# Final element's output projection in token halves with one PSUM bank for a block, and two output blocks between scores as row halves of the array

## The chip, the cores and the metric

The kernel runs on one core of a Trainium2 chip, in f32 throughout. The core has five engines that each run their own queue of instructions in program order: TensorE (PE; its weight loads are shown as PEld), VectorE (DVE), ScalarE (ACT), GpSimd (POOL) and SyncE (SP, which here only issues DMAs). The metric is the device time of one execution in microseconds (us); a kernel's time is the median of its runs.

## What is computed

The input is x with 8 batch elements of 512 channels and 32 x 32 = 1024 tokens. Two attention layers follow one another, each element on its own:

```python
# layer 0
hn  = group_norm(x, 32 groups)
q, k, v = split(w_qkv @ hn + b_qkv)            # 8 heads of 64 channels
wgt = softmax(q^T k / sqrt(64))                # 1024 x 1024 for each head
a   = wgt applied to v
x   = x + group_norm(w_proj @ a + b_proj)
# layer 1
q, k, v = split(weight_norm(v_qkv) @ x)        # each token normalised by its RMS over q, k and v
e   = exp(scores of q and k)                   # one head of 512 channels, 1024 x 1024
h   = (v applied to e) / sum(e)
out = (x + weight_norm(v_out) @ h) / sqrt(2)
```

## The kernel before

**Tiles.** Channels lie on the partitions: 512 channels are 4 blocks (`CI`) of `P` = 128 rows, and the 1024 tokens are two halves of `HN` = 512 or 8 blocks (`NT`) of 128. Each element passes through layer 0 in `STEPS` = 32 steps, a step being the scores of two heads for one token block, and then through layer 1 (`Layer1`, from line 912). `B` = 8 elements run one after the other.

**PSUM.** Two pools hold matmul results: three buffers of two banks (`wide`, and the scores) and two buffers of one bank (`bank`). A bank is 128 x 512 f32. A tile is taken from a pool in rotation, so a matmul into a new tile waits until the tile that had the buffer two or three takes ago has been read. In the rows of the profile `s` are score tiles, `pq` and `pqk` the projections of q and k, `po` outputs of attention (of both layers), `pp` the final element's output projection, `py` the products with the Gram matrix at the start of layer 1.

**Big buffers in SBUF.** Seven large slots are handed out first come, first served. `big(name)` takes one and `slots.give(name)` gives it back. Weight buffers that change owner with the stage are `near[name]`; `place(name, b)` takes such a place again and `fetch` issues its load on SP.

**Order.** Each engine's instructions stay in the order in which the program issues them, so the order of the Python calls is the order of the work. All operations go through one helper, which is why every row of the profile says L34.

**One step of layer 0** (`Heads.step`, line 630): `softmax(i)` (VectorE takes the negated maximum `nm` of both score tiles, ScalarE the exponential `p`), then every second step `values` of five steps ago, then the calls in `fill`, then the scores of the next step, then `turn` (VectorE transposes the scaled p of the step before into `pb`, and SP issues four DMAs that move it into `pT`), then `scale` (VectorE reciprocal, GpSimd two multiplications of p), then the calls in `later`. What `fill` holds is therefore TensorE work placed between two sets of scores. Score matmuls, and the projections called pq, use half of the array's rows each: two matmuls with 64 rows of contraction, one on the upper half of the rows and one on the lower. The output blocks `po` of layer 1 use all 128 rows.

**The passage from one element to the next.** The last part of layer 1 multiplies v by e for the second half of the tokens: four blocks of 128 channels, `products(1, c)` (line 1076), each eight logical matmuls into one bank. `keep(1, c)` (line 1085) follows: VectorE multiplies the bank by `sums`, the reciprocals of the exponentials' sums, then adds x times 2^-0.5 and stores into x, and SP sends the block out. Block 0 is done before the next element's heads begin. Blocks 1, 2 and 3 are handed to the first steps of the next element's heads: `fills` (line 1386) puts `products(1, c)` ahead of the scores of the step, `laters` (line 1387) puts `keep(1, c)` at its end. This happens seven times. Where there is a next element, the multiplication's result `share` lies in SBUF (`near["v#"]`), in the rows called `t` or `v`.

**The last element's layer 0.** There is no next element that could fill the gaps. While the last heads run, `project_out_half` (line 651) puts the projection of the first two channel blocks of `a` plus bias into `o`. After the loop of 32 steps (lines 1326 to 1340) come `values(14)`, `heads.turn()` with the last transpose and its DMAs, the load of the scores' weights, `OutBegun` (line 660), which starts the third channel block's share of the projection (ci = 2) for three of four output blocks in two-bank tiles, two loads of x, `values(15)`, and `finish_last` (line 671). The latter adds the fourth channel block's share (ci = 3) and finishes the remaining output block. For each output block, both token halves at once, it adds the tile to o (VectorE), takes statistics (two `bn_stats`) and aggregates them. Then it fetches `gram`, forms the GroupNorm coefficients a and c in a chain of small steps, and for each channel block ScalarE scales o and VectorE adds it to x. Layer 1's `project` (line 912) follows with py.

**The end.** After the last element's layer 1 the four blocks `products(1, c)` and `keep(1, c)` run in a row, without heads beside them (line 1395); here the multiplication's result stays in PSUM. Each block is sent with one DMA of 512 KB.

Of the kernel before, what the change touches and what calls it, by code (L numbers as in the profile page):

```python
# [18 lines left out]
G1S, G1B, BQ, BK, BV, BP, G2S, G2B, GQKV, GOUT, NCOLS = 0, 4, 8, 12, 16, 20, 24, 28, 32, 44, 48  # L19
# [33 lines left out]
def attention_blocks_kernel(  # L53
# [36 lines left out]
    ov = out.rearrange("b (ci p) h w -> b p ci (h w)", p=P)  # L90

    const = ctx.enter_context(tc.tile_pool(name="const", bufs=1))
    slots = Slots(ctx.enter_context(tc.tile_pool(name="slots", bufs=1)), "s", 7)
# [5 lines left out]
    small = ctx.enter_context(tc.tile_pool(name="small", bufs=3))  # L99
    tiny = ctx.enter_context(tc.tile_pool(name="tiny", bufs=1))  # L100
# [4 lines left out]
    PE, VE, AC, PO, SY = (InOrder(tc, e) for e in (nc.tensor, nc.vector, nc.scalar, nc.gpsimd, nc.sync))  # L105
# [5 lines left out]
    def wide(name):  # L111
        return ps_s.tile([P, 2, HN], F32, tag="sc", name=name)
# [4 lines left out]
    def matmuls(pm, terms):  # L117

        for k, (lhsT, rhs) in enumerate(terms):
            PE.matmul(pm, lhsT, rhs, start=(k == 0), stop=(k == len(terms) - 1))  # L120
            if k % 2:
                yield

    def run(pieces):
        for _ in pieces:
            pass
# [24 lines left out]
    def load_x(b, xt, ci):  # L151
        SY.dma_start(out=xt[:, ci, :], in_=xv[b, :, ci, :])
# [116 lines left out]
    def fetch(name, b):  # L269
        SY.dma_start(out=place(name, b), in_=far[name])  # L270
# [16 lines left out]
    def gn_stats(st, src, k):  # L287
        VE.bn_stats(st[:, k, :], src[:, k * HN : (k + 1) * HN])

    class GroupNorm:  # L290


        def __init__(self, mv, n, g0, b0, name, bank=bank):
            self.mv, self.n, self.g0, self.b0, self.name, self.bank = mv, n, g0, b0, name, bank
# [352 lines left out]
    def out_terms(a, j, th, cis):  # L647
        hs = slice(th * HN, (th + 1) * HN)
        return [(near["proj"][:, ci, j * P : (j + 1) * P], a[:, ci, hs]) for ci in cis]
# [7 lines left out]
                AC.activation(o[:, j, th * HN : (th + 1) * HN], pm, AF.Identity, bias=col(BP, j))  # L657
            yield

    class OutBegun:  # L660


        def __init__(self, b, h):
            self.pm = {}
            for j in range(CI - 1):
                self.pm[j] = wide(f"pp_{b}_{j}")
                for th in range(2):
                    for lhsT, rhs in out_terms(h.a, j, th, [CI // 2]):
                        PE.matmul(self.pm[j][:, th, :], lhsT, rhs, start=True, stop=False)

    def finish_last(b, h, xt, o, begun):

        def project_out(j, th, pm):
            terms = out_terms(h.a, j, th, range(CI // 2, CI))
            if j in begun.pm:
                PE.matmul(pm[:, th, :], *terms[1], start=False, stop=True)
            else:
                run(matmuls(pm[:, th, :], terms))  # L680

        st = tiny.tile([P, CI, 2, 6], F32, tag="gn_st2", name=f"st2_{b}")
        mv = small.tile([P, CI, 2], F32, tag="gn_mv2", name=f"mv2_{b}")
        for j in range(CI):
            pm = begun.pm[j] if j in begun.pm else wide(f"pp_{b}_{j}")
            for th in range(2):
                project_out(j, th, pm)
            VE.tensor_add(o[:, j, :], o[:, j, :], pm.rearrange("p a f -> p (a f)"))
            for k in range(2):
                gn_stats(st[:, j], o[:, j, :], k)  # L690
            VE.bn_aggr(mv[:, j, :], st[:, j])
        fetch("gram", b)
        norm = GroupNorm(mv, CI, G2S, G2B, f"2_{b}")
        norm.means()
        a, c = norm.coeffs()
        for j in range(CI):
            AC.activation(o[:, j, :], o[:, j, :], AF.Identity, bias=c[:, j : j + 1], scale=a[:, j : j + 1])
            VE.tensor_add(xt[:, j, :], xt[:, j, :], o[:, j, :])
        slots.give(f"a_{b}")
        slots.give(f"o_{b}")  # L700

    class RightSide:

# [197 lines left out]
    class Layer1:  # L901
# [174 lines left out]
        def products(self, th, c, between=None, po=None):  # L1076
# [4 lines left out]
            for k, _ in enumerate(matmuls(po, terms)):  # L1081
                if k == 1 and between:
                    between()

        def keep(self, th, c):

            hs = slice(th * HN, (th + 1) * HN)

            po = self.po.pop((th, c))
            share = near["v#"][:, N : N + HN] if self.b + 1 < B else po  # L1090
            VE.tensor_mul(share, po, self.sums[:, hs])
            VE.scalar_tensor_tensor(self.xt[:, c, hs], self.xt[:, c, hs], 2.0 ** -0.5, share, ALU.mult, ALU.add)
            if th == 1:
                SY.dma_start(out=ov[self.b, :, c, :], in_=self.xt[:, c, :])

# [135 lines left out]
    for b in range(B):  # L1231
# [77 lines left out]
        if more:  # L1309
            v0_next = big(f"v0_{b + 1}", NT)  # L1310
            v0 = project_v7(b + 1, right_v.columns, v0_next)
            Seven.hold()
            for _ in range(4):
                next(v0)
        heads.values(STEPS // RG - 2)
        heads.turn()
        if more:
            Seven.drain()
            fetch("proj7", b)
            ta = big(f"ta_{b}").rearrange("p (k i) (h n) -> p k i h n", k=2, h=2)  # L1320
            rhs = RightSide(heads.a, ta[:, 0], ta[:, 1])
            for j in range(CI // 2 + 1):
                rhs.sums(j)
            for _ in range(10):
                next(v0)
        else:
            fetch("score", b)
            begun = OutBegun(b, heads)
            for ci in (2, 3):
                load_x(b, xt, ci)  # L1330
        heads.values(STEPS // RG - 1)
        slots.give(f"v0_{b}")
        if more:
            xt = big(f"x_{b}")
            for ci in range(CI):
                load_x(b, xt, ci)
            fetch("gram", b)
            finish_layer0(b, heads, rhs, xt, v0)
        else:
            finish_last(b, heads, xt, o_last, begun)  # L1340
        fetch("value", b)
        one = Layer1(b, xt)
        one.project(hn_next)
# [36 lines left out]
        if more:  # L1380
            one.products(1, 0, norm_step)
            run(steps)
            one.keep(1, 0)
            heads = Heads(b + 1, hn_now, v0_next, qk_next)
            heads.scores(0)
            fills = [[lambda c=c: one.products(1, c)] for c in range(1, CI)] + [[]]
            laters = [[lambda c=c: one.keep(1, c)] for c in range(1, CI)] + [[]]

            def done(b=b):
                for name in (f"v1_{b}", f"e_{b}_1", f"x_{b}"):  # L1390
                    slots.give(name)

            laters[CI - 2].append(done)
        else:
            for c in range(CI):
                one.products(1, c)
                one.keep(1, c)


# [31 lines left out]
```

## Time and profile before

| | us |
|---|---|
| median of the 3 runs | 3225.41 (3222.88 to 3227.68) |
| the profiled execution's own time | 3224.11 |
| its span, from the first to the last instruction | 3222.0 |
| TensorE busy in it | 3192.6 |
| VectorE / GpSimd / ScalarE busy in it | 2279.2 / 1253.2 / 1045.5 |
| idle of TensorE before po<-pT,v, released by DMA pT<-pb | 3.0 |
| last TensorE instruction ends at | 3216.83 |

The mean TensorE clock granted in the span is 0.998 of full. A row of the profile names engine, operation, `out<-in` by the program's names with buffer numbers left out, the form (partitions x elements), and the count; a matmul's `64*128 64x512` is rows of contraction x output partitions, and the moving operand. One logical f32 matmul shows as two records on PE. Because matmuls are pipelined, a record's length overlaps the next record: the time from start to start is what a matmul costs. In a timeline the columns are start, busy time, engine, operation; a bracket gives the idle time before it and what ended that. Instructions of the same group that follow one another are put together, with x and their number.

### The profile page before, as it was taken

What the parts mean: (1) busy time and instruction counts of PE and PEld (TensorE: products, weight loads), DVE (VectorE), ACT (ScalarE), POOL (GpSimd) and SP (SyncE); (2) the same over time, 40 slices, a digit from 0 to 9 for tenths busy, and PEclk for the clock granted to TensorE, in tenths of its full rate; (3) what the DMA queues carried; (4) which work ended last, traced back from release to release, by engine and by line L of the source; (5) the groups of instructions that cost most, each with busy time, mean ns of one, the idle gap of its engine ahead of it and who ended that gap; (6) DMA issues with size and microseconds to landing.
All of it is one profiled execution on the core that took longest, in us unless ns stands there. A gap on an engine that the chain in (4) does not pass through costs nothing.

```text
span 3222.0 us, 36603 instructions
## 1 busy us (share of the span) xinstructions
PE 3192.6 (99%) x13218; PEld 1645.9 (51%) x13218; DVE 2279.2 (71%) x3166; ACT 1045.5 (32%) x1813; POOL 1253.2 (39%) x1025
## 2 busy tenths in 40 slices
PE   8999999999999999999999999999999999999899
PEld 5455644455444554545544555445554556444354
DVE  5697767876678765886658866587766877578652
ACT  2453114521145211551215512254023531145210
POOL 1554224732257212671227613265223642246121
PEclk9999999999999999999999999999999999999999
DMA  6777225862168512784228832388224872158600
GB/s 203 206 204 219 76 56 155 215 200 59 56 182 226 179 43 62 203 229 142 53 85 213 224 111 52 107 215 235 92 58 112 216 220 75 30 156 211 187 7 33
DMA packets 225180, 451.57 MB, mean 140 GB/s; under 512 B 21572, under 2 KB 62056, under 8 KB 219112
## 3 DMA queue, kind: packets, MB, share of 16 engines
q1 hardware_dynamic: 224880, 449.20, 49.7%
q8 instruction: 106, 1.74, 0.2%
q14 instruction: 74, 0.61, 0.1%
q10 hardware_dynamic: 120, 0.02, 0.0%
HBM read 137.26 MB, written 29.56 MB: 52 GB/s over the span
## 4 chain that ended last, share of the span: by engine, by line
PE 93%; DMA 3%; DVE 2%; SPq 1%; issue 1%; POOL 1%; DVEq 0%; ACTq 0%; POOLq 0%
PE po L34 26%; PE s L34 13%; PE pq L34 7%; PE p_e_T L34 7%; PE p_v_T L34 6%; PE p_e_B L34 5%; PE p_v_B L34 5%; PE pqk L34 4%; PE py L34 4%; PE p_u_T L34 3%; PE p_o_T L34 3%; PE p_u_B L34 3%; PE p_o_B L34 2%; DMA pT<-pb 2%; DVE pb L34 1%; PE pv L34 1%
## 5 line engine op out<-in xcount | busy, mean ns | idle before, releaser
L34 POOL TENSOR_SCALAR p<-p,tt 128x1024 f32<-128x1024 f32 x512 | 566.0, 1118 | 742.0 <-DVE tt L34 729.6
L34 ACT ACTIVATE p<-s,nm 128x1024 f32<-128x1024 f32 x512 | 565.6, 1109 | 876.3 <-DVE nm L34 534.0
L34 DVE TENSOR_REDUCE nm<-s 128x1 f32<-128x1024 f32 x512 | 602.2, 1217 | 151.7 <-PE s L34 151.0
L34 DVE STREAM_TRANSPOSE pb<-p 128x2048 f32<-128x2048 f32 x256 | 589.9, 2304 | 50.3 <-DMA pT<-pb 27.8
L34 PE MATMUL s<-qk 64*128 64x512 f32 x2048 | 524.0, 604 | 1.1 <-POOL qk L34 0.5
L34 PE MATMUL po<-pT,v 128*64 128x256 f32 x4096 | 471.8, 383 | 3.1 <-DMA pT<-pb 3.0
L34 PE MATMUL po<-e,v 128*128 128x512 f32 x1024 | 450.8, 596 | 0.0
L34 PEld LDWEIGHTS po<-pT,v 128*64 128x64 f32 x4096 | 285.1, 137 | 221.0 <-ACT v L34 31.8
L34 PEld LDWEIGHTS s<-qk 64*128 64x128 f32 x2048 | 200.5, 186 | 250.7 <-issue 222.2
L34 PEld LDWEIGHTS po<-e,v 128*128 128x128 f32 x1024 | 191.4, 190 | 241.1 <-issue 241.1
L34 PE MATMUL pq<-hn,qk 64*128 64x512 f32 x504 | 197.1, 592 | 0.0
L34 POOL TENSOR_TENSOR esum<-esum,e 128x512 f32<-128x512 f32 x96 | 130.5, 1360 | 154.3 <-ACT e L34 151.8
L34 POOL TENSOR_TENSOR u<-u,xy 128x512 f32<-128x512 f32 x64 | 79.2, 1268 | 280.9 <-DMA xy<-far_rinv 275.4
L34 POOL TENSOR_TENSOR x<-x,o 128x1024 f32<-128x1024 f32 x21 | 52.1, 2512 | 348.5 <-ACT o L34 348.5
L34 ACT ACTIVATE e<-e,shift,rinv 128x512 f32<-128x512 f32 x128 | 100.9, 812 | 256.7 <-DVE e L34 256.7
L34 DVE TENSOR_TENSOR e<-e,p_e_T 128x512 f32<-128x512 f32 x160 | 107.0, 685 | 86.5 <-PE p_e_T L34 84.3
L34 DVE TENSOR_TENSOR v<-v,p_v_T 128x256 f32<-128x256 f32 x300 | 114.3, 417 | 68.7 <-PE p_v_T L34 50.0
L34 PE MATMUL pqk<-hn,qk 64*128 64x512 f32 (+1 forms) x672 | 158.2, 590 | 0.0
L34 PE MATMUL pq<-v,qk 64*128 64x512 f32 x336 | 150.9, 589 | 0.0
L34 PE MATMUL pq<-t,qk 64*128 64x512 f32 x336 | 150.9, 589 | 0.0
L34 PE MATMUL p_e_T<-s,t 128*128 128x512 f32 x320 | 147.8, 592 | 0.0
L34 PE MATMUL py<-x,gram 128*128 128x512 f32 x320 | 140.3, 598 | 5.4 <-issue 5.4
(222 smaller groups left out, 4096.7 us busy)
## 6 DMA issues: line engine op xcount, KB each, us to landing
pT<-pb SPq DMA_DIRECT2D x1024, 256.0 KB, 4.6
qk<-far_qk SPq DMA_DIRECT2D x21, 896.0 KB
hn<-in_x_dram SPq DMA_DIRECT2D x32, 512.0 KB, 4.6
x<-in_x_dram SPq DMA_DIRECT2D x32, 512.0 KB, 3.6
out_dram<-x SPq DMA_DIRECT2D x32, 512.0 KB, 4.6
score<-far_score SPq DMA_DIRECT2D x8, 1792.0 KB
value<-far_value SPq DMA_DIRECT2D x8, 1792.0 KB
proj<-far_proj SPq DMA_DIRECT2D x7, 1792.0 KB
```

The costliest lines, as they stand in the source:

```text
L34: return lambda *args, **kw: self._pin(call(*args, **kw))
```

## The change

There are three parts.

**1. Row halves.** For the seven passages to a next element, blocks 2 and 3 of `products(1, c)` become `products_rows(c)`. Each matmul is split by rows of contraction: the upper 64 rows accumulate into one bank, the lower 64 into a second one, so that the block has 16 logical matmuls of 64 rows in place of 8 of 128, in the same form as the scores. `keep` then has two results to add: the first as before, the second by a ScalarE copy to SBUF and two GpSimd operations, a multiplication by `sums` and an addition into x. The output's DMA comes after that. Block 1 is unchanged.

**2. The last element's output projection in token halves.** `LastOut` takes the place of `OutBegun` and `finish_last`. Each output block of each token half has a bank of its own: half 0 in two tiles of two banks, half 1 in a tile of two banks and two tiles that use one of theirs. `first_half` runs both remaining channel blocks (ci = 2 and 3) for token half 0 right after the loop, ahead of `values(14)`, and `sums(0, 0)` (add, one `bn_stats`) stands ahead of `heads.turn()`. After the turn come the other three sums of half 0, and `begin_second` (ci = 2, half 1); after `values(15)`, `finish` adds ci = 3, with sums and aggregation for each block. `gram` gets a big slot of its own and is loaded earlier; the loads of x stand ahead of that of the scores' weights, which moves behind them. The last step over o and x runs in token halves.

**3. The last block of the last element.** Its first 512 columns, finished earlier, are sent before it; its second 512 columns are done in two pieces of 256 columns (`last_piece`), each with its own matmuls, its own multiplication and addition, and its own DMA of 128 KB.

```diff
-    class OutBegun:
+    class LastOut:
+        def __init__(self, b, h, o):
+            self.b, self.h, self.o = b, h, o
...
             self.pm = {}
-            for j in range(CI - 1):
-                self.pm[j] = wide(f"pp_{b}_{j}")
+        def banks(self, th, groups):
+            for js in groups:
+                t = wide(f"pp_{self.b}_{th}_{js[0]}")
+                for k, j in enumerate(js):
+                    self.pm[th, j] = t[:, k]
+        def share(self, th, j, ci, first):
+            for lhsT, rhs in out_terms(self.h.a, j, th, [ci]):
+                PE.matmul(self.pm[th, j], lhsT, rhs, start=first, stop=not first)
+        def first_half(self):
+            self.banks(0, ((0, 1), (2, 3)))
+            for j in range(CI):
+                self.share(0, j, CI - 2, True)
+                self.share(0, j, CI - 1, False)
+        def sums(self, th, j):
+            oh = self.o[:, j, th * HN : (th + 1) * HN]
+            VE.tensor_add(oh, oh, self.pm[th, j])
+            VE.bn_stats(self.st[:, j, th, :], oh)
+        def begin_second(self):
+            self.banks(1, ((0, 3), (1,), (2,)))
+            for j in range(CI):
+                self.share(1, j, CI - 2, True)
+        def finish(self, xt):
+            b, o = self.b, self.o
+            for j in range(CI):
+                self.share(1, j, CI - 1, False)
+                self.sums(1, j)
+                VE.bn_aggr(self.mv[:, j, :], self.st[:, j])
+            norm = GroupNorm(self.mv, CI, G2S, G2B, f"2_{b}")
+            norm.means()
+            a, c = norm.coeffs()
+            for j in range(CI):
                 for th in range(2):
-                    for lhsT, rhs in out_terms(h.a, j, th, [CI // 2]):
-                        PE.matmul(self.pm[j][:, th, :], lhsT, rhs, start=True, stop=False)
-    def finish_last(b, h, xt, o, begun):
...
-            VE.tensor_add(o[:, j, :], o[:, j, :], pm.rearrange("p a f -> p (a f)"))
-            for k in range(2):
-                gn_stats(st[:, j], o[:, j, :], k)
-            VE.bn_aggr(mv[:, j, :], st[:, j])
-        fetch("gram", b)
...
-            AC.activation(o[:, j, :], o[:, j, :], AF.Identity, bias=c[:, j : j + 1], scale=a[:, j : j + 1])
-            VE.tensor_add(xt[:, j, :], xt[:, j, :], o[:, j, :])
+                    hs = slice(th * HN, (th + 1) * HN)
+                    AC.activation(
+                        o[:, j, hs], o[:, j, hs], AF.Identity, bias=c[:, j : j + 1], scale=a[:, j : j + 1]
+                    )
+                    VE.tensor_add(xt[:, j, hs], xt[:, j, hs], o[:, j, hs])
...
+        def products_rows(self, c):
+            pos = self.po[1, c] = [bank(f"po1_{self.b}_1_{c}_{r}") for r in range(2)]
+            for t in range(NT):
+                for r in range(2):
+                    rows = halves[r]
+                    PE.matmul(
+                        pos[r],
+                        self.v[rows, t, c * P : (c + 1) * P],
+                        self.e[1][rows, t, :],
+                        start=(t == 0),
+                        stop=(t == NT - 1),
+                    )
         def keep(self, th, c):
-            po = self.po.pop((th, c))
+            po, rest = self.po.pop((th, c)), None
+            if isinstance(po, list):
+                po, rest = po
...
+            if rest is not None:
+                part = near["v#"][:, :HN]
+                AC.copy(part, rest)
+                PO.tensor_mul(part, part, self.sums[:, hs])
+                PO.tensor_add(self.xt[:, c, hs], self.xt[:, c, hs], part)
             if th == 1:
                 SY.dma_start(out=ov[self.b, :, c, :], in_=self.xt[:, c, :])
+        def last_piece(self, c, cols):
+            hs, po = slice(HN + cols.start, HN + cols.stop), bank(f"po1_{self.b}_1_{c}_{cols.start}", HN // 2)
+            run(matmuls(po, [(self.v[:, t, c * P : (c + 1) * P], self.e[1][:, t, cols]) for t in range(NT)]))
+            VE.tensor_mul(po, po, self.sums[:, hs])
+            VE.scalar_tensor_tensor(self.xt[:, c, hs], self.xt[:, c, hs], 2.0 ** -0.5, po, ALU.mult, ALU.add)
+            SY.dma_start(out=ov[self.b, :, c, hs], in_=self.xt[:, c, hs])
...
+        else:
+            last = LastOut(b, heads, o_last)
+            last.first_half()
+            last.sums(0, 0)
         heads.values(STEPS // RG - 2)
         heads.turn()
...
-            fetch("score", b)
-            begun = OutBegun(b, heads)
+            for j in range(1, CI):
+                last.sums(0, j)
+            last.begin_second()
+            near["gram"] = big(f"gram_{b}")[:, :, :C]
+            SY.dma_start(out=near["gram"], in_=far["gram"])
             for ci in (2, 3):
                 load_x(b, xt, ci)
+            fetch("score", b)
         heads.values(STEPS // RG - 1)
...
-            fills = [[lambda c=c: one.products(1, c)] for c in range(1, CI)] + [[]]
+            fills = [[lambda c=c: (one.products_rows(c) if c > 1 else one.products(1, c))] for c in range(1, CI)] + [[]]
...
-            for c in range(CI):
+            for c in range(CI - 1):
                 one.products(1, c)
                 one.keep(1, c)
+            SY.dma_start(out=ov[b, :, c + 1, :HN], in_=xt[:, c + 1, :HN])
+            for n in (0, HN // 2):
+                one.last_piece(c + 1, slice(n, n + HN // 2))
```

More of the change, by code (lines that the diff above doesn't have):

```diff
@@ L658, in project_out_half @@
             yield
-    class OutBegun:
-        def __init__(self, b, h):
-            self.pm = {}
-            for j in range(CI - 1):
-                self.pm[j] = wide(f"pp_{b}_{j}")
-                for th in range(2):
-                    for lhsT, rhs in out_terms(h.a, j, th, [CI // 2]):
-                        PE.matmul(self.pm[j][:, th, :], lhsT, rhs, start=True, stop=False)
-    def finish_last(b, h, xt, o, begun):
[L675 to L687, printed above, removed]
-            VE.tensor_add(o[:, j, :], o[:, j, :], pm.rearrange("p a f -> p (a f)"))
-            for k in range(2):
-                gn_stats(st[:, j], o[:, j, :], k)
-            VE.bn_aggr(mv[:, j, :], st[:, j])
-        fetch("gram", b)
[L693 to L696, printed above, removed]
-            AC.activation(o[:, j, :], o[:, j, :], AF.Identity, bias=c[:, j : j + 1], scale=a[:, j : j + 1])
-            VE.tensor_add(xt[:, j, :], xt[:, j, :], o[:, j, :])
-        slots.give(f"a_{b}")
-        slots.give(f"o_{b}")
@@ new lines, in attention_blocks_kernel @@
+    class LastOut:
+        def __init__(self, b, h, o):
+            self.b, self.h, self.o = b, h, o
+            self.st = tiny.tile([P, CI, 2, 6], F32, tag="gn_st2", name=f"st2_{b}")
+            self.mv = small.tile([P, CI, 2], F32, tag="gn_mv2", name=f"mv2_{b}")
+            self.pm = {}
+        def banks(self, th, groups):
[29 more added lines that the diff above has]
+            for j in range(CI):
+                for th in range(2):
+                    hs = slice(th * HN, (th + 1) * HN)
[3 more added lines that the diff above has]
+                    VE.tensor_add(xt[:, j, hs], xt[:, j, hs], o[:, j, hs])
+            slots.give(f"a_{b}")
+            slots.give(f"o_{b}")
@@ L1339, in attention_blocks_kernel @@
         else:
-            finish_last(b, heads, xt, o_last, begun)
+            last.finish(xt)
         fetch("value", b)
```

## The prediction

> **What bounds the kernel now.** I read the busy shares first, then the chain of waits, then the timeline at the places that the diff touches: the start of an element's heads, the end of the last element's first layer, and the last blocks.
>
> ```profile
> PE 3192.6 (99%) x13218; PEld 1645.9 (51%) x13218; DVE 2279.2 (71%) x3166; ACT 1045.5 (32%) x1813; POOL 1253.2 (39%) x1025
> ...
> PE 93%; DMA 3%; DVE 2%; SPq 1%; issue 1%; POOL 1%; DVEq 0%; ACTq 0%; POOLq 0%
> ```
>
> TensorE is the bound, so a microsecond counts only if TensorE gets it, or if it lies in the few stretches that are not its own. A logical f32 matmul is two records. Here is TensorE alone at the first heads of one element (start, length):
>
> ```profile
> 502.11 7.13 PE L34 MATMUL po<-e,v 128*128 128x512 f32 x16
> 509.17 1.99 PE L34 MATMUL s<-qk 64*128 64x512 f32 x8
> 511.09 7.13 PE L34 MATMUL po<-e,v 128*128 128x512 f32 x16
> 518.15 1.99 PE L34 MATMUL s<-qk 64*128 64x512 f32 x8
> 519.97 0.59 PE L34 MATMUL pq<-hn,qk 64*128 64x512 f32 x1
> ...
> 523.41 1.88 PE L34 MATMUL s<-qk 64*128 64x512 f32 x8
> 525.12 0.59 PE L34 MATMUL pq<-t,qk 64*128 64x512 f32 x1
> ```
>
> Starts are what to read. From pq at 519.97 to s at 523.41 is 3.44 us for 8 pairs of half-row records: 0.429 a pair. A whole-array record has the same pitch (py to the end: 112 po records in 48.16 us, 0.43). A block's 16 whole-array records, or its 16 half-row pairs, both want 6.87 us. But a po block between scores takes 7.06 (502.11 to 509.17), and s after it 1.92 (509.17 to 511.09) against 1.71 where half-row pq stands before and after (523.41 to 525.12). About 0.20 us goes at every change between halves and whole array.
>
> **Row-half blocks (7 elements, two blocks each).** Removed: four changes per element. From po at 502.11 to pq at 519.97 is 17.86; in halves it is 2 x 6.87 + 2 x 1.72 = 17.18, and the change into the first block (0.10 of it ahead of 502.11) goes too: 0.78 an element, 5.5 us in all. Added per block: 8 logical matmuls more, a second bank, one ScalarE copy (0.58, the row of v from pq), two GpSimd operations (1.27 each, the row v from v), and the output's DMA waits for GpSimd, not VectorE.
>
> Here a rule speaks against the change. The row says a pair costs what one whole record costs. The Trainium skill (TensorEngine Tiling (Array Packing), Instruction Overhead) charges each matmul some 60 cycles; at the 2.4 GHz of its TensorE page 224 extra records would cost 5.6 us and eat the gain. I take the row: the pq pairs carry the same shapes and show no such charge.
>
> Banks: block three needs both banks of block two. They come free about 0.7 us after it, scores between take 1.72: hidden, cover 1 us. SP: behind the delayed output DMA (some 3 us later) stands the next head's pT, issued at 515.79, when the DMA has gone at about 512.9; hidden.
>
> What is not hidden is the VectorE step that adds into x. It reads two operands from SBUF, and GpSimd's new multiply runs beside it:
>
> ```profile
> L34 DVE TENSOR_TENSOR t<-x x32: 681/685/1781, 340.8 to 3061.4; 128x512 f32<-128x512 f32 x32
> ...
> L34 DVE SCALAR_TENSOR_TENSOR x<-x,v x56: 691/692/843, 468.4 to 2854.9; 128x512 f32<-128x512 f32 x56
> ```
>
> These are min/median/max in ns. The long ones start while a GpSimd operation runs: at 518.99 the x step takes 0.84, GpSimd's hn operation ending at 519.29, 0.31 into it: what is left plus 0.54. The skill (SBUF — State Buffer, two separate sides) calls it an exclusive lock for whichever starts first, and the rows agree. Counted from the scores' first start, with the block's end at +0.18: VectorE's multiply to +0.89, its x step at +0.93; ScalarE's copy to +0.78, GpSimd at +0.86. GpSimd is first by 0.06 and holds until 2.13, so the x step ends at 2.67 in place of 1.62, and the maximum (nm) behind it on VectorE starts at 2.6, not when scores end at 1.9. In the step of block two TensorE has 6.87 us of block three to hide this. In the step of block three it hasn't:
>
> ```profile
> 521.49 1.11 ACT L34 ACTIVATE p<-s,nm 128x1024 f32<-128x1024 f32 x1 [6.68 <-DVE nm L34]
> ...
> 523.68 0.68 ACT L34 ACTIVATE qk<-pq,bqs 128x512 f32<-128x512 f32 x1
> 524.25 0.59 ACT L34 COPY qk<-pq 128x512 f32<-128x512 f32 x1
> ```
>
> That copy frees the bank of the second half of the next pq: it ends at 524.84, the pair starts at 525.12. nm started at 520.17, 2.02 after the scores; at 2.6 the copy ends at +7.3, the half can start at +7.44, and TensorE wants it at +6.87: 0.57 lost. That leaves 0.78 - 0.57 = 0.21 an element, 1.5 us. Whether GpSimd really wins in this step is near a toss-up, since its softmax scaling of the step before, late by the same 0.57, lets go only at about +0.93. Ends: loss 0 (VectorE first) to 0.57; nearest are the rows above, where GpSimd came first, so I take 0.57.
>
> **Last element's projection.** The timeline of the end of its heads:
>
> ```profile
> 3012.14 5.21 PE L34 MATMUL po<-pT,v 128*64 128x256 f32 x32 [2.59 <-DMA pT<-pb]
> 3012.93 2.31 DVE L34 STREAM_TRANSPOSE pb<-p 128x2048 f32<-128x2048 f32 x1 [2.34 <-POOL p L34]
> 3017.28 5.42 PE L34 MATMUL pp<-a,proj 128*128 128x512 f32 x12
> ...
> 3022.63 3.67 PE L34 MATMUL po<-pT,v 128*64 128x256 f32 x32
> 3026.23 8.85 PE L34 MATMUL pp<-a,proj 128*128 128x512 f32 x20
> ```
>
> TensorE waits 2.59 us for pT; its granted clock then is 0.50 until 3015.3, so 32 records take 5.14 to the next start, not 3.60. After 3028.25 VectorE sets the pace: four blocks of add 1.22, statistics 1.29, aggregate 0.21, ending at 3038.98. Now: first half (16 records, 6.97) from 3009.47, the old block's end, fills the wait; values at 3016.5; begin_second (8 records) at 3020.1; the last values at 3023.75. VectorE must first do sums(0, 0), and by the changed program's waits it starts when both blocks of that tile are written, 3013.2; 0.69 + 0.68 later the transpose runs, to 3016.85 in place of 3015.24. Its four DMAs landed 6.8 after it (3022.06), so now about 3023.7: just in time, cover 0.1. Values then end at 3027.45, the evacuation to a at 3028.1, and the first add starts at 3029.3. Per block add 0.69, statistics 0.68, aggregate 0.21, overlapped 1.56: four end at 3035.6, 3.4 earlier. The chain of small steps to c (4.57) is unchanged. Then halves: ScalarE 0.67 for 1.24, VectorE 0.68 for 1.22, 1.1 earlier to the first py. Sum 4.5. The gram load no longer waits for the last pp (3035.11), as it has its own slot; the loads behind it on SP are wanted from 3041 on. py starts at half clock in both.
>
> **End.** The last block's two 256-column pieces: 32 records at 0.2155 (p_v_T: 16 in 3.45) are 6.90 for 6.87. After them VectorE has 0.42 + 0.42 (rows of 128x256) for 0.70 + 0.69, and the last DMA is 128 KB for 512: before, 2.63 from issue to its wait's end, of which 1.35 moved data. An estimate from that: 0.7 saved, between 0 and 1.0. Sum 0.55 + 0.7 - 0.03 = 1.2.
>
> **Sum.** 1.5 + 4.5 + 1.2 = 7.2 us. The profiled execution took 3224.1 (span 3222.0): 3216.9. The median of the runs shown is 1.3 above it; 3225.4 - 7.2 = **3218.2**.
>
> **Rivals.** (1) VectorE takes SBUF first, or the late copy costs nothing: row halves keep 5.5 and the time is 3225.4 - 11.2 = 3214.2. For it: a lead of at most 0.06 us. Against: every overlapping case in the rows with GpSimd already running. (2) The projection gives little: pT of the last head lands later than 3023.7 and values wait, for instance by 2 us; or the row blocks lose all 5.5. 3220.5. For: its cover is 0.1. (3) **Slower**: the two halves don't run side by side. Then a block is 13.7 us, 14 of them add 96: 3225.4 + 96 - 5.5 - 5.7 = 3310. The only place in the trace like it is the pq at 497.63, whose second half waited for a bank, and lost 0.85. It decides from a pair pitch of 0.48 (11.2 us over 224 pairs), against 0.429 in pq of the same shapes. A smaller form, stalls of 1.6 us an element, also passes the line.
>
> **How the numbers follow.** Forecast 0.48, rival one 0.36, rival two 0.10, slower 0.06. The forecast alone is 3216 to 3220.5; with rival one and the DMA and clock bounds the range is 3212.4 to 3221.2. About 0.2% (6.5 us) can be told from no change: the line is 3219.0. The forecast is below it two times in three, rival one nearly always, rival two seldom: faster 0.68, same 0.26, slower 0.06.
>
> **What would show it.** After the change: po pairs at 0.43 with s, po, s unbroken; the x step at 1.7 us in row-half blocks, with a late second half of the following pq (forecast) or 0.69 (rival one); no wait of TensorE before values 14 and none at half clock there; statistics done 3.4 earlier relative to the end of values 13; py about 4.5 earlier; a DMA tail shorter by 0.7. Wrong would be a pitch over 0.43, values 15 waiting for pT, or a po block waiting for a bank.

## The result

| | us |
|---|---|
| before, median of 5 runs | 3226.09 (3222.88 to 3227.68) |
| changed, median of 5 runs | 3213.99 (3212.18 to 3214.67) |
| ratio | 0.9965, 95% interval 0.9954 to 0.9976 |
| changed once more, in a later set of 5 runs | 3213.43, ratio 0.9960, 0.9947 to 0.9972 |
| span of the profiled execution | 3210.3, before 3222.0 |

The change makes the kernel faster by 0.35% to 0.40%. The forecast was 3218.2; what came is the first rival, 3214.2, in which the row halves lose nothing. That the two figures agree so closely is partly luck: the three parts together give less than that rival counts (10.5 us for 11.2), and scatter made up the rest, as the table below shows. First the page of the changed kernel, busy time and chain of waits:

```profile
PE 3184.8 (99%) x13458; PEld 1649.0 (51%) x13458; DVE 2279.0 (71%) x3176; ACT 1058.2 (33%) x1831; POOL 1291.0 (40%) x1053
...
PE 93%; DMA 3%; DVE 2%; SPq 1%; issue 1%; POOL 0%; ACT 0%; DVEq 0%
```

TensorE is still the bound, with 7.8 us less busy time although it has 240 records more (224 of the row halves, 16 of the last block's pieces). To see where the 11.7 us of the span went, I compared the starts of the same work in the two traces: the first scores of each element's heads, the first `values` of its layer 0 (po<-pT), the first py of the last element, the last record of TensorE. A difference that arises between two such points belongs to the stretch between them. For one passage, and for the last element's values 13 and first py, the rows are (before, then changed):

```profile
488.64 1.99 PE L34 MATMUL s<-qk 64*128 64x512 f32 x8
530.37 3.67 PE L34 MATMUL po<-pT,v 128*64 128x256 f32 x32
3005.87 3.67 PE L34 MATMUL po<-pT,v 128*64 128x256 f32 x32
3046.15 1.19 PE L34 MATMUL py<-x,gram 128*128 128x512 f32 x1 [5.40 <-issue]
```

```profile
488.80 1.99 PE L34 MATMUL s<-qk 64*128 64x512 f32 x8
529.73 3.67 PE L34 MATMUL po<-pT,v 128*64 128x256 f32 x32
2999.09 3.67 PE L34 MATMUL po<-pT,v 128*64 128x256 f32 x32
3036.03 1.22 PE L34 MATMUL py<-x,gram 128*128 128x512 f32 x1 [4.39 <-DVE x L34]
```

| stretch | predicted | measured, two profiled executions |
|---|---|---|
| seven passages, row halves | 1.5 | 5.6: each of the seven 0.80 (41.73 before, 40.93 after) |
| last element, values 13 to first py | 4.5 | 3.3 (40.28 before, 36.94 after) |
| last TensorE work to the end of the span | 1.2 | 1.6 (5.19, 3.63) |
| everything else | 0 | 1.2, in steps of both signs |
| sum | 7.2 | 11.7 |

The 1.2 us of the last row are spread over places that the change does not touch, with steps between -1.1 and +0.9 us. Two executions of the changed kernel itself differ there by steps of the same size, for instance by 1.06 us at the fifth group of values of one element. Over all thirteen profiles (before, changed twice, and the ten experiments below) the stretches from the first values to the next layer's first py, summed over the first seven elements, lie between 1390.7 and 1396.8 us, and no part of the change is in them. I count the 1.2 us as scatter. It also sets what the medians below can tell: their intervals reach 2 to 5 us to each side, so smaller sizes are read from the passages in the traces.

**The passage.** The timeline of TensorE in the changed kernel, at the same place that the prediction showed of before (start, length). Upper and lower half are told apart by the order of the calls, upper first, and by which bank is read first:

```profile
497.78 2.40 PE L34 MATMUL pq<-hn,qk 64*128 64x512 f32 x7
499.60 0.59 PE L34 MATMUL s<-qk 64*128 64x512 f32 x1
500.03 0.59 PE L34 MATMUL pq<-hn,qk 64*128 64x512 f32 x1
500.03 1.87 PE L34 MATMUL s<-qk 64*128 64x512 f32 x6
501.32 0.59 PE L34 MATMUL po<-e,v 64*128 64x512 f32 x1
501.74 0.59 PE L34 MATMUL s<-qk 64*128 64x512 f32 x1
501.75 7.02 PE L34 MATMUL po<-e,v 64*128 64x512 f32 x30
508.19 0.59 PE L34 MATMUL s<-qk 64*128 64x512 f32 x1
508.61 0.59 PE L34 MATMUL po<-e,v 64*128 64x512 f32 x1
...
518.49 0.59 PE L34 MATMUL pq<-hn,qk 64*128 64x512 f32 x1
518.91 0.59 PE L34 MATMUL s<-qk 64*128 64x512 f32 x1
518.92 0.59 PE L34 MATMUL pq<-hn,qk 64*128 64x512 f32 x1
519.34 0.59 PE L34 MATMUL pq<-t,qk 64*128 64x512 f32 x1
```

Two things are to be read here. From the first row-half po (501.32) to the first pq (518.49) are 17.17 us, where the prediction wanted 17.18; a block's 16 upper records take 6.87 (501.32 to 508.19). And the two halves of the array do not run level. At 499.60 scores of the upper half start although a pq of the lower half follows at 500.03, and at 508.61 the last po of the lower half comes after the upper half's first score. The lower half is 0.85 us behind: 518.49 for the upper half's next projection, 519.34 for the lower's. The lag comes from the first pq, whose second half waits 0.85 us for a bank. Before, the whole-array block behind it waited for both halves, and the lag ended there. Now nothing needs both halves until `values`, and the lag is carried through two blocks.

What that does to the evacuation, the reading of the finished banks by the other engines, is seen in their timeline, block 2, changed kernel:

```profile
508.39 0.69 DVE L34 TENSOR_TENSOR v<-po,esum 128x512 f32<-128x512 f32 x1 [2.25 <-PE po L34]
509.12 0.69 DVE L34 SCALAR_TENSOR_TENSOR x<-x,v 128x512 f32<-128x512 f32 x1
509.29 0.59 ACT L34 COPY v<-po 128x512 f32<-128x512 f32 x1 [4.17 <-PE po L34]
509.96 1.27 POOL L34 TENSOR_TENSOR v<-v,esum 128x512 f32<-128x512 f32 x1 [1.49 <-ACT v L34]
510.11 2.36 DVE L34 TENSOR_REDUCE nm<-s 128x1 f32<-128x1024 f32 x2 [0.30 <-PE s L34]
```

VectorE takes the upper half's bank at 508.39, before the lower half's last record has started. ScalarE gets its bank 0.90 later, GpSimd starts at 509.96, and VectorE's x step has ended at 509.81. The two SBUF operations, the x step and GpSimd's multiplication, do not overlap, and over the whole run the x step is 0.69.

```profile
L34 DVE SCALAR_TENSOR_TENSOR x<-x,v x56: 691/692/693, 468.6 to 2847.1; 128x512 f32<-128x512 f32 x56
```

**The projection.** TensorE from the first half of the last output projection to the GroupNorm ahead of py, changed kernel:

```profile
3002.69 7.13 PE L34 MATMUL pp<-a,proj 128*128 128x512 f32 x16
3009.76 3.67 PE L34 MATMUL po<-pT,v 128*64 128x256 f32 x32
3013.36 3.70 PE L34 MATMUL pp<-a,proj 128*128 128x512 f32 x8
3018.01 3.67 PE L34 MATMUL po<-pT,v 128*64 128x256 f32 x32 [0.94 <-DMA pT<-pb]
3022.24 3.70 PE L34 MATMUL pp<-a,proj 128*128 128x512 f32 x8 [0.56 <-ACT a L34]
3029.78 0.56 PE L34 MATMUL pm<-mv,gavg 128*128 128x4 f32 x2 [3.84 <-DVE mv L34]
```

The wait ahead of values 14 is gone, and its 32 records take 3.60 to the next start at full clock. A new wait of 0.94 stands ahead of values 15, for pT; in a second profile of the same kernel it is 0.53.

### The profile page after: what moved, and what is told of

The parts are those of the page before. It is cut to its first block, busy times and chain, and to the rows that moved or that the text cites. A ratio compares the mean times of both kernels' runs of the same rounds, so it can differ in the third digit from the quotient of the medians.

```text
span 3210.3 us, 37159 instructions
## 1 busy us (share of the span) xinstructions
PE 3184.8 (99%) x13458; PEld 1649.0 (51%) x13458; DVE 2279.0 (71%) x3176; ACT 1058.2 (33%) x1831; POOL 1291.0 (40%) x1053
## 3 DMA queue, kind: packets, MB, share of 16 engines
q8 instruction: 108, 1.77, 0.2%
## 4 chain that ended last, share of the span: by engine, by line
PE 93%; DMA 3%; DVE 2%; SPq 1%; issue 1%; POOL 0%; ACT 0%; DVEq 0%
PE po L34 26%; PE s L34 13%; PE pq L34 7%; PE p_e_T L34 7%; PE p_v_T L34 6%; PE p_e_B L34 5%; PE p_v_B L34 5%; PE py L34 4%; PE pqk L34 4%; PE p_u_T L34 3%; PE p_o_T L34 3%; PE p_u_B L34 3%; DMA pT<-pb 2%; PE p_o_B L34 2%; DVE pb L34 1%; SPq L34 1%
## 5 line engine op out<-in xcount | busy, mean ns | idle before, releaser
L34 PE MATMUL s<-qk 64*128 64x512 f32 x2048 | 544.5, 603 | 0.7
L34 PE MATMUL po<-e,v 128*128 128x512 f32 (+2 forms) x1264 | 461.3, 587 | 0.0
L34 PEld LDWEIGHTS s<-qk 64*128 64x128 f32 x2048 | 210.9, 186 | 246.0 <-issue 216.6
L34 PEld LDWEIGHTS po<-e,v 128*128 128x128 f32 (+1 forms) x1264 | 201.4, 189 | 233.9 <-issue 233.1
```

The source lines that it names most:

```text
L34: return lambda *args, **kw: self._pin(call(*args, **kw))
```

## The experiments

The theory after the result: **the lag** of the lower half kept GpSimd behind VectorE, and gave the second half of the next projection 0.85 us that the forecast did not count. The rival: the forecast's lock does not exist in this form, or cannot reach TensorE, and the rows gain for another reason.

### Row halves alone, and in one block only

`rows_only` is before with part 1 of the change; `rows3_only` is the same with `c > 2` in place of `c > 1`, so that block 2 stays on the whole array.

```diff
-fills = [[lambda c=c: one.products(1, c)] for c in range(1, CI)] + [[]]
+fills = [[lambda c=c: (one.products_rows(c) if c > 1 else one.products(1, c))] for c in range(1, CI)] + [[]]
```

> The kernel before with the row-half blocks alone. If the rows keep all that the mode changes cost (theory of the lag: the lower half of the array runs 0.85 us behind the upper, so GpSimd starts behind VectorE's x step), each passage starts its first values 0.80 us earlier and the time falls by 5.6 us, to a ratio of about 0.9983. If the extra of the whole change came from elsewhere, by the forecast's lock, the passages give 0.21 each and the time falls by 1.5.

> The kernel before with block 3 alone in row halves, block 2 on the whole array. If the gain is the changes between halves and whole array at 0.20 us each, two of four go and a passage gives 0.39, 2.7 us in all. If it is the carrying over of the 0.85 us by which the lower half lags, or another effect of both blocks together, block 2 on the whole array brings the halves level again and a passage gives nothing or the full 0.8.

Measured: rows_only 3217.62 against 3225.59 (ratio 0.9974, 0.9965 to 0.9984); in its trace every one of the seven passages gives 0.80 (one 0.79). rows3_only 3221.31 (0.9989, 0.9982 to 0.9996); every passage gives 0.40. The medians fell by more than the passages account for, 8.0 for 5.6 and 4.3 for 2.8; the intervals reach down to both, and the rest is not explained. So two changes between halves and whole array are worth 0.40, four are worth 0.80, and the lag itself is neither won nor lost: it is paid at the first whole-array work, be that a block or `values`. The forecast's 0.78 an element was right, and its loss of 0.57 did not occur.

### The two halves brought level again

`resync` puts the first term of block 3 on the whole array, into the upper half's bank, so that both banks of that block end together. The diff leaves out two lines that let the lower half's bank begin with the second term.

```diff
             for t in range(NT):
+                if t == 0 and c == CI - 1:
+                    PE.matmul(pos[0], self.v[:, t, c * P : (c + 1) * P], self.e[1][:, t, :], start=True, stop=False)
+                    continue
...
```

> The changed kernel with the first term of block 3 on the whole array, which brings the two halves level again before the step whose copies the next projection waits for. Cost in any case: two mode changes of 0.20, 2.8 us over seven passages. Theory of the lag: now both banks end together, VectorE's x step and GpSimd's multiply come within 0.1 us of each other; where GpSimd is first the x step takes about 1.7 and the second half of the next projection starts 0.57 late, 4.0 us more, so plus 6.8 in all; where VectorE is first plus 2.8. If lag and lock play no part: plus 2.8 and an x step of 0.69.

Measured: 3216.50 (0.9973, 0.9961 to 0.9985), each passage 0.40 later than in the changed kernel. The step after block 3:

```profile
517.41 1.88 PE L34 MATMUL s<-qk 64*128 64x512 f32 x8
517.61 0.69 DVE L34 TENSOR_TENSOR v<-po,esum 128x512 f32<-128x512 f32 x1 [3.48 <-PE po L34]
517.71 0.59 ACT L34 COPY v<-po 128x512 f32<-128x512 f32 x1 [4.60 <-PE po L34]
518.34 0.69 DVE L34 SCALAR_TENSOR_TENSOR x<-x,v 128x512 f32<-128x512 f32 x1
518.38 1.77 POOL L34 TENSOR_TENSOR v<-v,esum 128x512 f32<-128x512 f32 x1 [1.94 <-ACT v L34]
519.33 2.36 DVE L34 TENSOR_REDUCE nm<-s 128x1 f32<-128x1024 f32 x2 [0.30 <-PE s L34]
```

Here is the level case that the forecast worked with. VectorE is first by 0.04 us, and the one held up is GpSimd: 1.77 for 1.27 (1.77 or 1.78 in all seven passages, while VectorE's x step stays at 0.69). The forecast had GpSimd first by 0.06. So one engine does hold up the other; who is first was called near a toss-up, and it fell to VectorE. The 0.40 lost are the two changes of mode alone.

### GpSimd made first

`resync_late` delays VectorE by one small copy from the same bank in block 3.

```diff
+            if rest is not None and c == CI - 1:
+                VE.tensor_copy(small.tile([P, CI], F32, tag="gn_ve", name=f"late_{self.b}"), po[:, :CI])
             VE.tensor_mul(share, po, self.sums[:, hs])
```

> The kernel resync (halves level ahead of block 3's step; there VectorE's x step began 0.04 us before GpSimd's multiply and held it up, 1.77 in place of 1.27) with one small VectorE copy of 0.15 us from the same bank ahead of VectorE's multiply, so that GpSimd is first. By the forecast's arithmetic: x step about 1.7, maximum 0.9 later than in resync, second half of the next projection 0.6 to 0.75 late, 4 to 5 us over seven passages on top of resync's plus 2.8. If the lock cannot reach TensorE: x step longer, but the first values of each passage no later than in resync.

Measured: 3220.24 (0.9982, 0.9975 to 0.9989), every passage 0.61 or 0.62 later than in resync. The same step:

```profile
517.16 1.88 PE L34 MATMUL s<-qk 64*128 64x512 f32 x8
518.12 1.27 POOL L34 TENSOR_TENSOR v<-v,esum 128x512 f32<-128x512 f32 x1 [1.94 <-ACT v L34]
518.15 1.78 DVE L34 SCALAR_TENSOR_TENSOR x<-x,v 128x512 f32<-128x512 f32 x1
519.86 2.34 DVE L34 TENSOR_REDUCE nm<-s 128x1 f32<-128x1024 f32 x2
```

A lead of 0.03 us for GpSimd turns 0.69 into 1.78, which is what is left of GpSimd's operation (1.24) plus 0.54, as the forecast had it; it is 1.78 in all seven passages. The maximum starts 2.70 after the scores (517.16), in resync 1.92. So with level halves and GpSimd first the loss is 0.61 a passage, of which the small copy can be 0.06, by which the x step starts later after the scores; the forecast said 0.57. Its price was right, its case did not occur.

### GpSimd first, with the lag

`swap` keeps the lag and gives VectorE the lower half's bank, the late one.

```diff
-                po, rest = po
+                rest, po = po
```

> The changed kernel with the two banks of a row-half block exchanged in the evacuation: VectorE takes the lower half's bank, ScalarE and GpSimd the upper's, which is ready 0.85 us earlier. Theory of the lag with the lock: GpSimd's multiply now starts about 0.1 us before VectorE's, the x step takes about 1.0 to 1.5 us in place of 0.69 and the maximum starts up to 0.9 later; the lag leaves the second copy 0.85 us of slack, so the time rises by 0 to 1.8 us only. If there is no lock, the x step stays at 0.69.

Measured: 3210.94 (0.9953, 0.9938 to 0.9968). Timelines of GpSimd and of VectorE in the step after block 3, swap:

```profile
517.33 1.27 POOL L34 TENSOR_TENSOR v<-v,esum 128x512 f32<-128x512 f32 x1
```

```profile
518.14 1.01 DVE L34 SCALAR_TENSOR_TENSOR x<-x,v 128x512 f32<-128x512 f32 x1
519.07 1.21 DVE L34 TENSOR_REDUCE nm<-s 128x1 f32<-128x1024 f32 x1
```

The x step is held up, here for 0.32, and it also starts later, because its bank is the late one. The maximum starts 2.70 after the upper half's scores (516.37), in the changed kernel 1.93 (516.77 to 518.70). That is the same 2.70 as in resync_late. Even so the passages take what they took in the changed kernel, 40.93 in each of the seven, where resync_late lost 0.61. The first records of the upper half's next projection are 0.04 to 0.15 later after its scores than in the changed kernel, those of the lower half are not, and as the lower half is 0.85 behind anyway, only it sets the end. The median was expected 0 to 1.8 us above the changed kernel's and is 3 us under it, but the intervals overlap and no passage shows it; I do not count swap as a gain. So a maximum that is late by almost 0.8 costs 0.61 a passage with level halves, and nothing with the lag.

### The wait for pT

`turnfirst` moves the first sum of half 0 behind the transpose (first diff); `gramlate` issues gram's load behind values 15 (second diff).

```diff
             last.first_half()
-            last.sums(0, 0)
         heads.values(STEPS // RG - 2)
         heads.turn()
...
-            for j in range(1, CI):
+            for j in range(CI):
                 last.sums(0, j)
```

```diff
-            near["gram"] = big(f"gram_{b}")[:, :, :C]
-            SY.dma_start(out=near["gram"], in_=far["gram"])
...
         heads.values(STEPS // RG - 1)
...
+            near["gram"] = big(f"gram_{b}")[:, :, :C]
+            SY.dma_start(out=near["gram"], in_=far["gram"])
             last.finish(xt)
```

> The changed kernel with the last transpose ahead of the first sum of LastOut instead of behind it. If the 0.94 us that TensorE waits for pT before values 15 comes from VectorE's late transpose, it starts 1.4 us earlier, pT lands before TensorE is ready, the wait goes and the time falls by 0.9 us. If VectorE's other sums are then late for the banks of the second half, the wait moves to begin_second.

> The changed kernel with the load of gram issued behind values 15 instead of right behind pT's four DMAs. From the last transpose's end to pT's landing the changed kernel takes 7.71 us, the kernel before 6.82. If the load of gram crowds pT, the landing comes 0.8 us earlier and so do values 15, 0.85 us less in all. If it is the spread of the DMAs alone, the landing stays near 7.7 after the transpose or moves by chance, and the time stays.

Measured: turnfirst 3210.87 (0.9957, 0.9942 to 0.9972), gramlate 3211.72 (0.9958, 0.9944 to 0.9973). In gramlate pT lands 7.70 after the transpose's end, in the changed kernel 7.71 (7.30 in its second profile): nothing points to gram's load. In turnfirst TensorE does not wait, and values 15 start 1.0 earlier. Across all profiles the time from the last transpose's end to the landing of the fourth DMA lies between 6.79 and 9.21 us: 6.82, 7.97 and 6.79 in the three with the old projection, 7.17 to 9.21 in the ten with the new. Whether the new order of loads also makes it somewhat later on average, three profiles of the old one cannot tell. The forecast took the 6.82 of one execution and called 0.1 us its cover.

But turnfirst's profile keeps none of its 1.4 us (1.0, and 0.4 in the small steps). p_u_T, the product with the scores' weights, follows py; its first record comes 59.1 us after values 13, and 59.2 in the changed kernel's first profile. Windows of its TensorE (stretch, length, busy time and records, granted clock, DMA) show where they went:

```profile
3028.03:3031.44 3.41, 0.00 (x0) 0.50 0.01 4
3031.44:3034.86 3.42, 2.49 (x3) 0.50 0.00 0
3034.86:3038.27 3.41, 3.41 (x5) 0.50 0.00 0
3038.27:3041.68 3.41, 3.41 (x9) 1.00 0.00 0
```

py starts at 3032.37, and the clock comes back at 3038.27: 5.9 us of py at half clock. In the changed kernel it was 3.1 (3036.03 to 3039.15). In these profiles the clock changes on a grid of 3.41 us. Here a stretch of the grid that was busy for 2.49 us was not followed by full clock; the next, busy throughout, was. Where the grid lies against the kernel differs from profile to profile, so an earlier py does not shorten the stretch by itself.

### TensorE kept busy

`warm` puts matmuls whose results nobody reads into the gap of the GroupNorm: three logical ones behind the last output block, four behind pv. `turnwarm` has four and four, and turnfirst's order. Here pm and pv are the two small matmuls of the GroupNorm. The diff is that of warm.

```diff
+        def warm(self, n):
+            pm = bank(f"warm_{self.b}_{n}")
+            for k in range(n):
+                for lhsT, rhs in out_terms(self.h.a, 0, 0, [0]):
+                    PE.matmul(pm, lhsT, rhs, start=(k == 0), stop=(k == n - 1))
...
+            self.warm(3)
             norm = GroupNorm(self.mv, CI, G2S, G2B, f"2_{b}")
             norm.means()
             a, c = norm.coeffs()
+            self.warm(4)
```

> The changed kernel with matmuls whose results nobody reads in the gap of the last element's GroupNorm: three logical ones behind the last output block, four behind pv. The granted clock there is 0.50 from 3028.9 to 3039.15, of which 3.1 us are py. If idleness of TensorE sets it, the clock stays full, py runs 1.55 us shorter, pm and pv together 0.14, and the time falls by 1.7 us. If it is something else, or the extra matmuls delay pm or py, no gain or a loss up to 0.5.

> The changed kernel with both: the last transpose ahead of the first sum of LastOut, and four logical matmuls whose results nobody reads behind the last output block and four behind pv. Theory of idle windows: the clock stays at full through the GroupNorm gap, the stretch from the first py to the first p_u_T takes 20.5 us or less, against 22.2 to 23.7 in the runs so far; with values 15 about 1 us earlier and the small steps 0.4 shorter the time falls by 3.0 to 4.5 us against the changed kernel, to a ratio of about 0.995 to before. If the clock gives back what the earlier transpose gains, as in turnfirst, 0 to 1.

> The changed kernel itself once more, on the same chip and with the same runs of before as turnwarm. If the 3 us between it (3213.99 in its first runs) and the kernel with the two banks exchanged (3210.94) lie in the day's chip and in the phase of the clock's windows, it comes out at 3211 to 3214; in the profile the stretch from the first py to the first p_u_T lies anywhere between 22.2 and 23.7, and values 15 wait 0.3 to 1.2 us for pT.

Measured: warm 3209.22 (0.9949, 0.9932 to 0.9965), turnwarm 3210.10 (0.9948, 0.9935 to 0.9962), the changed kernel beside it 3213.43 (0.9960, 0.9947 to 0.9972). From the first py to the first p_u_T:

| kernel | us |
|---|---|
| changed, first profile / again | 22.23 / 23.59 |
| turnfirst / gramlate | 23.62 / 23.66 |
| warm / turnwarm | 20.60 / 20.70 |

warm lost the clock for one stretch of the grid, before py; the unread matmuls then ran at half clock and held py up by 0.7 us (2.28 from the first scaling of o to py, 1.59 in turnwarm). In turnwarm the clock did not fall before the last TensorE work. Windows of 3.40 us, which need not lie on the grid:

```profile
3028.10:3031.50 3.40, 3.40 (x9) 1.00 1.00 426
3031.50:3034.90 3.40, 2.26 (x8) 1.00 0.29 122
3034.90:3038.30 3.40, 2.55 (x7) 1.00 0.00 0
3038.30:3041.70 3.40, 3.40 (x9) 1.00 0.00 0
```

Its stretch is 1.5 to 2.9 us shorter than the changed kernel's, though not quite the 20.5 that was expected. Its pT landed 9.21 us after the transpose, the latest of all, so that values 15 waited 0.86 in spite of the earlier transpose. turnwarm is 3.3 us under the changed kernel in the same set of runs and faster than before beyond doubt; against the changed kernel the intervals overlap, and what is shown is the shorter stretch.

### The other two parts without row halves

`last_only` is the changed kernel with the old `fills`.

```diff
-fills = [[lambda c=c: (one.products_rows(c) if c > 1 else one.products(1, c))] for c in range(1, CI)] + [[]]
+fills = [[lambda c=c: one.products(1, c)] for c in range(1, CI)] + [[]]
```

> The changed kernel without row halves: all blocks of the passages on the whole array, the last element's projection and end as in the change. If the parts add up as the two traces showed it, projection 3.4 (2.5 to 4.0 with the spread of pT's landing and of the clock's windows) and end 1.55 give 4.9 us less than before, and every passage's first values stand where they did; last engine work to the end of the span is 3.6 us.

Measured: 3219.24 against 3224.59 (0.9984, 0.9977 to 0.9991), 5.4 less. In its profile the passages do not move, the stretch from the last element's values 13 to py gains 3.3, and from the last TensorE work to the end of the span it takes 3.67. Read from the traces the parts add up: 5.6 of the passages, 3.3 and 1.5, which makes 10.4, against 10.5 for the same three stretches in the changed kernel. The medians (8.0 for rows_only, 5.4 here, 11.2 to 12.1 for the whole) agree with that within their intervals and no more closely.

## Why the prediction was right, and where it was wrong

**The range held and the sign was right; the likeliest case was not what came.** The rival with 0.36 was. It named two ways to come true, VectorE first or a late copy that costs nothing; what it did not have is the reason, the lag.

1. **Pitch of the row halves, 0.429 a pair: right.** 16 pairs take 6.87 in the changed kernel. By the prediction's estimate from the rule of the Trainium skill (TensorEngine Tiling (Array Packing), Instruction Overhead) the 224 extra records would have added 5.6 us; nothing of it is seen. The page adds that a matmul with a free dimension of 1 takes as long as one of 60, so it may mean a least time, which 512 columns would not feel.
2. **Four mode changes, 0.78 an element: right,** 0.80, and 0.40 for two of them.
3. **The loss of 0.57 by the lock: wrong; the rows gave 5.6 for 1.5.** The step that failed is "Counted from the scores' first start, with the block's end at +0.18". It set one end for both banks. The lower half ends 0.85 later, and the trace of before showed why: the pq at 497.63, whose second half waited for a bank. The prediction named that row, as a lost 0.85, but for another rival, and did not ask where the lag goes once no whole-array block ends it. With it, ScalarE's copy and GpSimd come 0.85 later, and the second half of the projection is wanted 0.85 later. The second of these is enough by itself: with GpSimd made first under the lag nothing was lost (swap). And the order was misjudged even for level halves, where VectorE came first (resync). The price itself, 0.57, was near what it costs where it does apply (0.61).
4. **Banks and SP: right.** No po block waits for a bank; block 3's output DMA goes at 521.18, ahead of the next pT at 523.33.
5. **The filled wait and the clock at values 14: right.** Values 14 start 10.67 after values 13, predicted 10.63 (3016.5 less 3005.87).
6. **pT in time for values 15: mis-sized.** 0.94 waited, 0 predicted. The landing varied between 6.8 and 9.2 us and was taken from one execution; the rival that named this wait gave it 2 us. The statistics were then done 2.6 earlier, not 3.4.
7. **Small steps and halves to py: 0.86 for 1.1.** From pm to py 7.11 became 6.25. pm now ran at half clock; the steps from pm to c took 4.62 for 4.48.
8. **"py starts at half clock in both": held, but by the draw of the grid,** 3.28 us before and 3.12 after; the changed kernel had 5.8 in its second profile.
9. **The end: mis-sized within its bounds.** From VectorE's last work (ending 3218.30 before, 3207.61 after) to the end of the span 3.7 became 2.7, so the stretch with the smaller DMA saved 1.0, where 0.7 was taken between 0 and 1.0. VectorE's share was as predicted, 0.55 (1.43 from its last multiplication's start before, 0.88 after).

## What to carry to other kernels

Where neighbouring work uses halves of the array, put the work between it into the same halves too: each change of mode avoided gives 0.2 us here, and a wait of one half does not stop the other at once. Before pricing a collision of two engines in hundredths of a microsecond, follow the halves separately: a wait of one half earlier in the trace shifts everything that hangs on it. And a gain in front of a stretch that starts at half clock is not a gain until the clock is settled. Matmuls whose results nobody reads kept the clock up in turnwarm's one profile; without them the stretch from py to p_u_T moved by up to 1.4 us by chance.

## What the runs showed of the hardware that was not expected

- **The two row halves overtake each other.** Scores of the upper half run while earlier matmuls of the lower half are still to start (508.19 and 508.61), over two blocks and two sets of scores, with a constant lag of 0.85 us. Here the order of the program held only within a half, and VectorE read the bank of one half (508.39) while the other half still had a record to start (508.61).
- **The hold-up between VectorE and GpSimd works both ways and turns on hundredths.** VectorE first by 0.04: GpSimd takes 1.77 for 1.27. GpSimd first by 0.03: VectorE takes 1.78 for 0.69. In both cases the one that is held up ends about 0.15 us sooner than if it had only begun when the first was done: VectorE 0.54 after GpSimd's end where its step takes 0.69, GpSimd 1.12 after VectorE's end (519.03 to 520.15 in resync) where it takes 1.27.
- **The clock's grid.** Stretches of 3.41 us. In the thirteen profiles, grid stretches with 1.42 us of TensorE work or less were followed by half clock (the 1.42 is warm's), those with 1.51 (turnfirst) or more were not; half clock ended only after stretches with at least 3.1 us of work (the changed kernel's), and not after 2.34, 2.43, 2.49 or 2.58. The Trainium skill (TensorE: Matmul & The Clock Gate, Part 1: The HAM clock gate) says that the window is free-running and about 3.4 us long; the profiles agree, and add these shares.
- **The landing of the last of pT's four transfers scatters** from 6.79 to 9.21 us after the end of the transpose that releases them, in thirteen profiles.
